# Graph convolution sums by ranked adding gathers in place of dense adjacency products

## The chip, the cores and the metric

The kernel runs on one core of a Trainium2 chip. TensorE (PE) multiplies matrices, VectorE (DVE) and ScalarE (ACT) do elementwise work, GpSimd (POOL) does elementwise work and issues indirect DMAs, SyncE (SP) issues most plain DMAs. The metric is the device time of one execution in microseconds (us). The kernel before takes 2163.23 us, the median of three runs (2161.73 to 2163.58).

## The reference

A small graph network over N = 2500 nodes with 256 features and E = 40000 directed edges, the edges sorted by their destination. Two blocks follow each other. The first adds a SAGE convolution (the mean over a node's incoming edges) and a linear attention to `x`, then a mixture of eight experts. The second is where the change lies: a two-layer GCN convolution and a stack of four linear-attention layers work on the same normalised rows, both are added to `x`, and a second mixture of experts closes the kernel.

```python
xn = _layernorm(x, axis=-1)
x = x + _L1_gnn_ref(xn, edge_index, ...) + _L1_mix_ref(xn[None], ...)[0]
x = x + _L1_ffn_ref(_layernorm(x, axis=-1)[None], ...)[0]
```

The GCN convolution, `_L1_gnn_ref`:

```python
def _gcn_aggregate(h, src, dst, norm, b, n):
    msg = h[src] * norm[:, None]
    agg = jax.ops.segment_sum(msg, dst, num_segments=n)
    return agg + b
n = x.shape[0]
loops = jnp.arange(n, dtype=edge_index.dtype)
src = jnp.concatenate([edge_index[0], loops])
dst = jnp.concatenate([edge_index[1], loops])
deg = jax.ops.segment_sum(jnp.ones_like(dst, dtype=x.dtype), dst, num_segments=n)
dis = jnp.where(deg > 0, jax.lax.rsqrt(jnp.maximum(deg, 1e-12)), 0.0)
norm = dis[src] * dis[dst]
h = _gcn_aggregate(x @ W1, src, dst, norm, b1, n)
h = jnp.where(h >= 0, h, alpha * h)
h = _gcn_aggregate(h @ W2, src, dst, norm, b2, n)
```

Each node sums the rows of its neighbours and its own row, scaled on both sides by `dis`, twice, with a product by a 256 x 256 matrix ahead of each sum.

## The kernel before

Nodes are cut into 20 tiles of 125 (`NT`, `P`), five groups of four tiles (`NG`, `GT`; a group has `GC` = 500 nodes). The work runs in stages, one after the other.

- **Loading and probing the edges**, to about 86 us of the span. `count_edges` gives each node its number of edges.
- **Build**, 86 to 305 us. For each group of destination nodes, one-hot products build the piece of the adjacency matrix (how often each of 2500 sources reaches each of the 500 nodes) in `edges`, in bf16. `neighbours` (line 292) multiplies it by the node table, which is held in three bf16 terms so that the sum is good to float32: 20 source tiles x 2 halves of 128 features x 3 terms = 120 matmuls of 374 ns for a group. A callback `between(k)` builds the next group's piece in between, and steps other generators (the routing's gates) along. The result is copied out by DVE and ACT (line 750, `aT`) and goes through the SAGE products. Here SP also writes each piece, with the identity added for the self loops (DVE, line 753), to `adj` in DRAM, 2500 x 2500 numbers in bf16.
- **Routing and the first mixture**, to 555 us: the tokens are scattered to their experts' rows of `sorted0` by POOL (line 407), and 47 tiles of 128 rows go through the experts from 356 us on (lines 813 to 850), 3.83 us each. SP loads each tile's expert weights (`wt`, four buffers) and rows (`xs`) ahead.
- **`first_norm`**, 555 to 628 us: layer-norm of all rows, and `conv_in`, the convolution's first 256 x 256 product scaled by `dis`. It writes the rows to `tab1` in DRAM and splits them in three bf16 terms (`split3`: ACT and POOL) to `table`.
- **Four attention layers**, `attention(l)`, 628 to 1678 us. Each computes keys, `context_out` (lines 982 to 1001), scores, and the feed-forward products `ffn(g)` for the five groups (lines 1148 to 1171). `conv_1(g)` (line 924) stands before `ffn` in these layers: groups 0 and 1 in layer 0, groups 2, 3 and 4 in layers 1, 2 and 3. It loads the pieces of `adj` on SP (four buffers, one DMA for two source tiles), does `neighbours`, scales by `dis` along the rows (`along_rows`, lines 273 to 282), applies the bias and the leaky unit, and does the second 256 x 256 product (`conv_in`, the products at line 914).
- **`conv_2`** (line 945), 1678 to 1813 us: the second sum, 600 matmuls with `adj` pieces again, transposed back and added to `X`.
- **Gates, sort and the second mixture**, to the end. The rows sorted for it lie in `sorted1`, which is an alias of `adj`'s memory; they are scattered by POOL (line 407) and gathered by POOL (line 1345).

Each engine runs its instructions in program order; the order across engines is set by semaphores that the tile framework places from the reads and writes of each buffer. If more edges fall on a place than a fixed window holds, `lost` is 1 and a loop of plain gathers computes the sums instead; the given edges don't need it.

Of the kernel before, what the change touches and what calls it, by code (L numbers as in the profile page):

```python
# [9 lines left out]
F32 = mybir.dt.float32  # L10
I32 = mybir.dt.int32
# [21 lines left out]
KC = 2  # L33
# [17 lines left out]
def gps_kernel(ctx: ExitStack, tc: tile.TileContext, a, out):  # L51
# [69 lines left out]
    ones = const.tile([P, 128], F32, name="ones")  # L121
    V.memset(ones, 1.0)
# [11 lines left out]
    adj = dram.tile([NG, P, NT, GC], BF16, name="adj")  # L134
    kth = scan.tile([128, 128], BF16, name="kth")
    G.iota(kth, pattern=[[1, 128]], base=0, channel_multiplier=0, allow_small_or_imprecise_dtypes=True)
    identb = scan.tile([P, P], BF16, name="identb")
    V.tensor_copy(identb, ident[:P, :P])
# [24 lines left out]
    begin = probe.tile([P, NQ], I32, name="begin")  # L163
# [47 lines left out]
    cnt = const.tile([P, NT], F32, name="cnt")  # L211

    def count_edges(pool):
# [15 lines left out]
        counts = dram.tile([N], F32, name="counts")  # L229
        nc.sync.dma_start(counts.rearrange("(q m n) -> m q n", q=NQ, n=BD), per)  # L230
        byrow = pool.tile([NT, P], F32, name="byrow")
        nc.sync.dma_start(byrow, counts.rearrange("(i p) -> i p", p=P))
        pc = psum2.tile([P, NT], F32, tag="cx", name="pc")
        T.transpose(pc, byrow, ident[:NT, :NT])
        V.tensor_copy(cnt, pc)
        return lost

    def gather_sums(pool, acc, table):
# [6 lines left out]
        gh = pool.tile([128, CH], F32, name="gh")  # L245
        V.tensor_scalar(gh, ge[:, :, 1], 1.0 / P, -0.496, ALU.mult, ALU.add)
        V.tensor_scalar(gh, gh, MAGIC, -MAGIC, ALU.add, ALU.add)
        gf = pool.tile([128, CH], F32, name="gf")
        V.tensor_copy(gf, ge[:, :, 1])
        V.scalar_tensor_tensor(gf, gh, -float(P), gf, ALU.mult, ALU.add)  # L250
        gs = pool.tile([128, CH], I32, name="gs")
        V.scalar_tensor_tensor(gs, gf, float(NT), gh, ALU.mult, ALU.add)
# [20 lines left out]
    def along_rows(pool, v, g):  # L273

        ps = psum2.tile([128, GC], F32, tag="ag", name="ps")
        for k in range(GT):
            dg = pool.tile([P, P], F32, tag="dg", name="dg")
            V.tensor_scalar(dg, ident[:P, :P], v[:, g * GT + k:g * GT + k + 1], None, ALU.mult)
            T.matmul(ps[:, k * P:(k + 1) * P], ones, dg, start=True, stop=True)
        row = pool.tile([128, GC], F32, tag="row", name="row")  # L280
        S.copy(row, ps)
        return row

    def neighbours(g, table, piece, between=None, banks=None):


        pa = banks or [psum2.tile([128, GC], F32, tag="ag", name=f"pa{c}") for c in range(2)]
        for k in range(NT):
            e = piece(k)
            for c in range(2):  # L290
                for n in range(3):
                    T.matmul(pa[c], table[:, k, n, c * 128:(c + 1) * 128], e,  # L292
                             start=(k == 0 and n == 0), stop=(k == NT - 1 and n == 2))
            if between is not None:
                between(k)
        return pa
# [238 lines left out]

    sorted1 = adj.rearrange("g p k d -> (g p k d)").bitcast(F32)[0:NE // 2 * N * RW].rearrange("(r c) -> r c", c=RW)
# [75 lines left out]
    with tc.tile_pool(name="lay0", bufs=1) as lay0:  # L612
# [91 lines left out]
        degrees(cnt)  # L704
# [5 lines left out]
        with tc.tile_pool(name="build", bufs=1) as build:  # L710
# [15 lines left out]

            ahead = new_edges()
            for k in range(GT):
                build_tile(ahead, 0, k)
            for g in range(NG):  # L730
                edges = ahead
                for lo, hi in ((0, g * GT), ((g + 1) * GT, NT)):
                    if hi > lo:
                        move(nc.sync, adj[g][:, lo:hi, :], edges[:, lo:hi, :])
# [5 lines left out]
                def between(k):  # L740
# [3 lines left out]
                    if gating is not None and k in (7, 15):  # L744
                        next(gating)

                pa = neighbours(g, xb, lambda k: edges[:, k, :], between)
# [3 lines left out]
                for k in range(GT):  # L751
                    o = edges[:, g * GT + k, k * P:(k + 1) * P]
                    V.tensor_tensor(o, o, identb, ALU.add)
                move(nc.sync, adj[g][:, g * GT:(g + 1) * GT, :], edges[:, g * GT:(g + 1) * GT, :])
# [22 lines left out]
    n_lost = nc.values_load(lost[0:1, 0:1], min_val=0, max_val=1)  # L777
    with tc.tile_pool(name="lost0", bufs=1) as pool, tc.For_i(0, n_lost, 1):
# [8 lines left out]
        nc.sync.dma_start(tab0.rearrange("(p k) d -> p k d", p=P), acc[:, :, :D])  # L787
# [78 lines left out]
    with tc.tile_pool(name="big", bufs=4) as big, tc.tile_pool(name="hid", bufs=8) as hid, \  # L866
# [30 lines left out]
        tab1 = dram.tile([N, D], F32, name="tab1")  # L897
        terms2 = dram.tile([NG, P, GT, 3, D], BF16, name="terms2")
        table = conv.tile([P, NT, 3, D], BF16, name="table")
        dval = const.tile([P, NT], F32, name="dval")  # L900
        V.tensor_scalar(dval, dis, valid, None, ALU.mult)

        def conv_in(g, src, w, keep):

            for b in range(0, GT, 2):
                i = g * GT + b
                if keep and b:
                    t = conv.tile([P, 3, D], F32, tag="t3", name="t3")[:, 0:2, :]
                else:
                    t = conv.tile([P, 2, D], F32, tag="t", name="t")  # L910
# [5 lines left out]
                if keep:  # L916
                    move(nc.sync, tab1.rearrange("(p k) d -> p k d", p=P)[:, i:i + 2, :], t)
                    split3(table[:, i:i + 2], t, G)
                else:
                    t3 = conv.tile([P, 2, 3, D], BF16, tag="t3", name="t3")  # L920
                    split3(t3, t, G)
                    move(nc.sync, terms2[g][:, b:b + 2], t3)

        def conv_1(g):
# [11 lines left out]
            for c in range(2):  # L936
                V.tensor_tensor(u[:, c, :], pa[c], row, ALU.mult)
# [551 lines left out]
```

## Time and profile before

| what | us |
|---|---|
| median of three runs | 2163.23 (2161.73 to 2163.58) |
| the profiled execution's own time | 2163.04 |
| its span | 2161.2 |
| mean granted clock of TensorE | 0.960 |
| layer 0 from `context_out` on, two groups of `conv_1` | 661.4 to 957.9 |
| layer 1 from `context_out` on, one group of `conv_1` | 957.9 to 1218.1 |
| layer 2 from `context_out` on, one group of `conv_1` | 1218.1 to 1478.3 |
| last group's `ffn` of layer 0, of layer 1, of layer 3 ends | 897.6, 1157.8, 1678.2 |
| `conv_2`'s matmuls | 1678.2 to 1807.2 |
| first product of the next stage (line 1254) | 1819.5 |

The profile counts from the first instruction. Its groups of instructions read: line, engine, operation, what it writes from what, and the count, then the busy time of all, the mean duration in ns, and the idle time of the engine just before them with what ended it. "issue" means that the profile shows nothing that the engine waited for. A clock of 1.00 is TensorE's full speed. A DMA that POOL issues shows as a POOL instruction of about 1 us; its data lands later.

### The profile page before, as it was taken

To read this page: it belongs to the slowest core of one execution; us is meant where nothing else is said; L and a number is where in the kernel's file an instruction comes from. 1 tells how busy PE (TensorE), PEld (TensorE's weight loads), DVE (VectorE), ACT (ScalarE), POOL (GpSimd) and SP (SyncE) were. 2 spreads that over 40 slices of the span, in tenths; PEclk is the share of its full clock that TensorE was granted. 3 is DMA by queue.
4 is the path that set the end of the run, shared out by engine and by line. 5 is a ranking of instruction groups with operands and counts; after the bars stand their busy time and mean duration, and the time that the engine had idled before them with its cause. 6 is when DMAs were issued, how large, how long until landed. Compare 5 with 4: busy or idle time off the path is not lost. (4 is left out here: it accounts for less than half of the span.)

```text
span 2161.2 us, 25307 instructions
## 1 busy us (share of the span) xinstructions
PE 1959.8 (91%) x9035; PEld 1309.3 (61%) x9035; DVE 896.2 (41%) x2822; ACT 580.8 (27%) x989; POOL 315.6 (15%) x288
## 2 busy tenths in 40 slices
PE   2699973999689999999999999999999998995996
PEld 2556643887466577676676767666676443334665
DVE  6866542333644346435463443635441023212333
ACT  1433201222361222223323133232322000331220
POOL 2302322222130201001010010000211000122222
PEclk9799986999799999999999999999999999997999
DMA  4022445665512200111001100022100435111100
GB/s 121 9 81 71 110 144 165 200 198 175 139 39 66 70 6 13 35 43 38 0 13 42 50 24 0 13 63 77 29 0 1 126 95 183 36 28 33 33 19 24
DMA packets 83119, 141.30 MB, mean 65 GB/s; under 512 B 18700, under 2 KB 64254, under 8 KB 82227
## 3 DMA queue, kind: packets, MB, share of 16 engines
q1 hardware_dynamic: 66193, 112.35, 17.7%
q0 software_dynamic: 13840, 20.89, 3.5%
q10 hardware_dynamic: 2949, 6.33, 1.1%
q8 instruction: 76, 1.25, 0.2%
q14 instruction: 61, 0.49, 0.1%
HBM read 103.85 MB, written 37.61 MB: 65 GB/s over the span
## 5 line engine op out<-in xcount | busy, mean ns | idle before, releaser
L1166 PE MATMUL mm<-w,h 128*125 128x256 f32 x1280 | 286.1, 379 | 0.0
L1156 PE MATMUL mm<-xT,w 128*128 128x500 f32 x640 | 282.9, 582 | 0.0
L1166 PEld LDWEIGHTS mm<-w,h 128*125 128x125 f32 x1280 | 239.2, 188 | 43.0 <-issue 9.2
L292 PEld LDWEIGHTS <-table 125*128 125x128 bf16 x1200 | 117.1, 98 | 126.7 <-issue 1.7
L1156 PEld LDWEIGHTS mm<-xT,w 128*128 128x128 f32 x640 | 119.0, 190 | 109.2 <-issue 100.8
L1159 ACT ACTIVATE h<-mm,bf 128x500 f32<-128x500 f32 x160 | 107.6, 677 | 216.6 <-PE mm L1156 216.5
L1151 POOL TENSOR_TENSOR tok<-tok,b 125x1024 f32<-125x1024 f32 x20 | 47.3, 2364 | 684.5 <-DVE tok L1143 632.4
L292 PE MATMUL pa<-piece,table 125*128 125x500 bf16 x600 | 138.1, 374 | 0.0
L292 PE MATMUL pa<-edges,xb 125*128 125x500 bf16 x600 | 134.4, 377 | 1.7 <-ACT edges L725 1.7
L292 PE MATMUL mm<-piece,table 125*128 125x500 bf16 x600 | 127.3, 374 | 0.0
L1167 DVE TENSOR_TENSOR tok<-tok,mm 125x256 f32<-125x256 f32 x80 | 33.5, 419 | 206.8 <-PE mm L1166 178.7
L1394 PE MATMUL py<-wd,taken 128*128 x432 | 96.9, 381 | 10.0 <-DVE taken L1384 10.0
L828 PE MATMUL mm<-xc,wt 128*128 128x128 f32 x752 | 97.1, 283 | 7.6 <-DVE idx L834 4.0
L828 PEld LDWEIGHTS mm<-xc,wt 128*128 128x128 f32 x752 | 89.6, 194 | 18.0 <-DVE xc L824 12.9
L292 PEld LDWEIGHTS <-xb 125*128 125x128 bf16 x600 | 58.2, 100 | 64.0 <-issue 4.1
L842 PE MATMUL py<-w,h 128*128 x376 | 96.1, 382 | 0.9 <-ACT h L832 0.9
L1394 PEld LDWEIGHTS py<-wd,taken 128*128 128x128 f32 x432 | 81.2, 190 | 25.3 <-DVE taken L1384 13.1
L832 ACT ACTIVATE h<-mm,wt 128x128 f32<-128x128 f32 x188 | 53.8, 369 | 137.6 <-issue 127.3
L357 ACT ACTIVATE xT<-mm,mixc 128x500 f32<-128x500 f32 x80 | 58.9, 768 | 116.1 <-PE mm L352 82.0
L725 ACT CAST edges<-mm 125x500 bf16<-125x500 f32 x100 | 64.7, 784 | 89.4 <-PE mm L722 80.3
L1254 PE MATMUL mm<-xTf,w 128*128 128x500 f32 x160 | 79.2, 618 | 6.0 <-DMA w<-in_L_ffn_W_dram 6.0
L1067 PE MATMUL mm<-xT,wa 128*128 128x500 f32 x160 | 76.4, 622 | 3.9 <-ACT xT L357 3.9
(363 smaller groups left out, 2833.6 us busy)
## 6 DMA issues: line engine op xcount, KB each, us to landing
wt<-in_expert_in_dram SPq DMA_DIRECT2D x47, 514.0 KB
piece<-adj SPq DMA_DIRECT2D x100, 218.8 KB
w<-in_L_mix_W_dram SPq DMA_DIRECT2D x8, 1024.0 KB
wd<-in_L_ffn_Wd_dram SPq DMA_DIRECT2D x8, 1024.0 KB
xs<-sorted SPq DMA_DIRECT2D x47, 130.0 KB
w<-in_L_ffn_W_dram SPq DMA_DIRECT2D x8, 512.0 KB
adj<-edges SPq DMA_DIRECT2D x2, 1750.0 KB
terms<-t SPq DMA_DIRECT2D x10, 336.0 KB
```

The source lines that it names most:

```text
L292: T.matmul(pa[c], table[:, k, n, c * 128:(c + 1) * 128], e, start=(k == 0 and n == 0), stop=(k == NT - 1 and n == 2))
L357: S.activation(o, ps, AF.Identity, bias=shift[:, c:c + 1], scale=gain[:, c:c + 1])
L725: S.copy(o.rearrange("p s (n d) -> p n s d", d=BD), ps[:P].rearrange("p (n s d) -> p n s d", n=BD, d=BD))
L828: T.matmul(ps[:, j * TS:(j + 1) * TS], wt[:, c * F0 + j * 128:c * F0 + (j + 1) * 128], xc[:, c * TS:(c + 1) * TS], start=(c == 0), stop=(c ...
L832: S.activation(h[:, j * TS:(j + 1) * TS], ps[:, j * TS:(j + 1) * TS], AF.Gelu, bias=wt[:, 2 * F0 + j:2 * F0 + j + 1])
L842: T.matmul(ps, h[:, j * TS:(j + 1) * TS], w2[:, ds(e, 1), j, :], start=(j == 0), stop=(j == NJ - 1))
L1067: T.matmul(ps, wk[:, kc, c * 128:(c + 1) * 128], hT[:, kc, g * GC:(g + 1) * GC], start=(kc == 0), stop=(kc == 1))
L1156: T.matmul(ps, w1[:, c, j * 128:(j + 1) * 128], fT[:, c, g * GC:(g + 1) * GC], start=(c == 0), stop=(c == 1))
L1159: S.activation(h, ps, AF.Gelu, bias=bf[:, l, j:j + 1])
L1166: T.matmul(ps, hh[j][:, k * P:(k + 1) * P], w2[:, j, :], start=(j == 0), stop=(j == nj - 1))
L1254: T.matmul(ps, w1[:, c, j * 128:(j + 1) * 128], xT[:, c, g * GC:(g + 1) * GC], start=(c == 0), stop=(c == 1))
L1394: T.matmul(ps, h[:, j * TS:(j + 1) * TS], wd[:, ds(e, 1), j, :], start=(j == 0), stop=(j == nj - 1))
```

## The change

The adjacency matrix is still built in `edges` for the first block, but no longer stored. The GCN sums are done by indirect DMAs that add in their destination.

`rank_nodes`, a generator stepped along in the build stage, ranks the nodes by their number of edges, the most first, by counts on DVE and two products for each group. Each node's number, its first edge and its `dis` are scattered to its rank's row of `byrank` (20 scatters on POOL), loaded back (`byr`), and 20 gathers bring the edges of each rank's node, as many as its tile's entry of `MOST`, to `wins`. `hit` tells which of them belong to the node; the others point to row N of the table, which is zero.

`gather` walks the 20 tiles of 128 ranked nodes, four at a time in turn. For each tile the first gather brings the nodes' own rows to `acc`, and each further one adds the row of one more neighbour: 20 plain and 349 adding gathers for one convolution by the sum of `MOST`. Each gather to a tile of `acc` waits for the tile's gather before it. `between(j)` then scales, adds the bias and applies the leaky unit; `to_nodes` scatters the tile's rows to the next table, `tabs[1]`, or to `sums2`. The second sum runs on rows before their product by `W2`, which `conv_out` does for all rows behind the layers. `conv_step(now)` places `between` in the programs of ACT and DVE: `LAYER` and `AHEAD` say how many gathers are reckoned to be done by a point of a layer, and every tile that is due by then is emitted there.

On DVE's program this puts three tiles' `between` after layer 0's third group, four at layer 0's end, four after the second and four after the fourth group of layer 1, four at its end, and the last after `context_out` of layer 2. On POOL it puts all 369 gathers of the first sum first, then the 20 scatters `to_nodes`, then the second sum's gathers.

Besides: `sorted1` has memory of its own, cleared by five SP DMAs from a tile of zeros (one stands ahead of the `lost` loop; four come in SP's order amid the first mixture's loads, two of them together after some 27 tiles, and one each four tiles later); the adds of `ffn` (lines 1151 and 1171) move from POOL to DVE; the loads of `b2` and `gm` move from POOL's queue to ACT's; the second fallback loop has its own flag `lost1`, one more value loaded to registers; the first fallback's table is laid out by node.

The core of the diff:

```diff
-KC = 2
+MOST = (42, 24, 22, 21, 20, 19, 18, 18, 17, 16, 16, 15, 15, 14, 14, 13, 13, 12, 11, 9)
+LAYER = 182
+AHEAD = 20
+NBIN = 64
...
-    adj = dram.tile([NG, P, NT, GC], BF16, name="adj")
...
+    def rank_nodes(pool):
+        bins = pool.tile([P, NBIN], F32, name="bins")
+        G.iota(bins, pattern=[[-1, NBIN]], base=NBIN - 1, channel_multiplier=0, allow_small_or_imprecise_dtypes=True)
+        upto = pool.tile([P, NT], F32, name="upto")
+        V.tensor_scalar(upto, cnt[:, 0:NT], float(NBIN - 1), None, ALU.min)
+        oh = pool.tile([P, NT, NBIN], F32, name="oh")
+        V.tensor_tensor(oh, bins[:, None, :].to_broadcast([P, NT, NBIN]), upto[:, :, None].to_broadcast([P, NT, NBIN]), ALU.is_equal)
+        full = pool.tile([128, NBIN], F32, name="full")
+        V.memset(full, 0.0)
+        rank = pool.tile([P, NT, NBIN], F32, name="rank")
...
+        at = pool.tile([P, NT], I32, name="at")
+        with nc.allow_low_precision("sums of one integer and zeros"):
+            V.tensor_reduce(at, rank, AX.X, ALU.add)
...
+        byrank = dram.tile([NT * 128, 4], F32, name="byrank")
...
+            made.append(G.indirect_dma_start(
+                out=byrank, out_offset=bass.IndirectOffsetOnAxis(ap=at[:, i:i + 1], axis=0), in_=rec[:, i, :], in_offset=None,
+            ))
...
+        byr = pool.tile([128, NT, 4], F32, name="byr")
+        nc.sync.dma_start(byr, byrank.rearrange("(j p) c -> p j c", p=128))
...
+        wins = pool.tile([128, heads_of[NT], 2], I32, name="wins")
+        hit = pool.tile([128, heads_of[NT]], F32, name="hit")
+        for j in range(NT):
+            part = slice(heads_of[j], heads_of[j + 1])
+            G.indirect_dma_start(
+                out=wins[:, part, :].rearrange("p e t -> p (e t)"), out_offset=None, in_=pairs,
+                in_offset=bass.IndirectOffsetOnAxis(ap=from_[:, j:j + 1], axis=0),
+            )
+            V.tensor_scalar(hit[:, part], wins[:, part, 0], byr[:, j, 0:1], None, ALU.is_equal)
...
-    sorted1 = adj.rearrange("g p k d -> (g p k d)").bitcast(F32)[0:NE // 2 * N * RW].rearrange("(r c) -> r c", c=RW)
+    sorted1 = dram.tile([NE // 2 * N, RW], F32, name="sorted1")
...
+            ranking = rank_nodes(build)
...
-                for lo, hi in ((0, g * GT), ((g + 1) * GT, NT)):
-                    if hi > lo:
-                        move(nc.sync, adj[g][:, lo:hi, :], edges[:, lo:hi, :])
...
+                    if g > 0 and k in (3, 11, 19):
+                        next(ranking, None)
...
-                    V.tensor_tensor(o, o, identb, ALU.add)
-                move(nc.sync, adj[g][:, g * GT:(g + 1) * GT, :], edges[:, g * GT:(g + 1) * GT, :])
...
-                if keep:
-                    move(nc.sync, tab1.rearrange("(p k) d -> p k d", p=P)[:, i:i + 2, :], t)
-                    split3(table[:, i:i + 2], t, G)
-                else:
-                    t3 = conv.tile([P, 2, 3, D], BF16, tag="t3", name="t3")
-                    split3(t3, t, G)
-                    move(nc.sync, terms2[g][:, b:b + 2], t3)
...
+                move(nc.sync, by_node(tabs[0])[:, i:i + 2, :], t)
...
-            row = along_rows(conv, dis, g)
-            pa = neighbours(g, table, piece)
-            u = conv.tile([128, 2, GC], F32, tag="u", name="u")
-            for c in range(2):
-                V.tensor_tensor(u[:, c, :], pa[c], row, ALU.mult)
-            for c in range(2):
-                neg = conv.tile([128, GC], F32, tag="row", name="neg")
-                V.tensor_scalar(neg, u[:, c, :], bcol[:, 0, c:c + 1], 0.0, ALU.add, ALU.min)
-                S.activation(u[:, c, :], u[:, c, :], AF.Relu, bias=bcol[:, 0, c:c + 1])
-                V.scalar_tensor_tensor(u[:, c, :], neg, alpha, u[:, c, :], ALU.mult, ALU.add)
-            conv_in(g, u, wc2, False)
...
+        def gather(tab, then, counted):
+            def one(j, k):
+                by = node[:, j:j + 1] if k == 0 else nbr[:, heads_of[j] + k - 1:heads_of[j] + k]
+                more = {} if k == 0 else {"compute_op": ALU.add}
+                counted()
+                return G.indirect_dma_start(out=acc[:, j, :], out_offset=None, in_=tab,
+                                            in_offset=bass.IndirectOffsetOnAxis(ap=by, axis=0), **more).ins
+            at = {j: 0 for j in range(4)}
+            coming = 4
+            wait = []
+            while at:
+                for j in list(at):
+                    ins = one(j, at[j])
+                    at[j] += 1
+                    wait = [(i, n - 1) for i, n in wait]
+                    while wait and wait[0][1] <= 0:
+                        then(wait.pop(0)[0])
+                    if at[j] > MOST[j]:
+                        del at[j]
+                        wait.append((j, 4))
+                        if coming < NT:
+                            at[coming] = 0
+                            coming += 1
+            for i, _ in wait:
+                then(i)
+            return ins
...
+        def to_nodes(tab, j):
+            G.indirect_dma_start(
+                out=tab, out_offset=bass.IndirectOffsetOnAxis(ap=node[:, j:j + 1], axis=0), in_=acc[:, j, :], in_offset=None,
+                bounds_check=N - 1, oob_is_err=False,
+            )
+        def between(j):
+            o = acc[:, j, :]
+            b = conv.tile([128, D], F32, tag="b", name="b", bufs=2)
+            S.activation(b, b1row, AF.Identity, scale=disr[:, 0, j:j + 1])
+            V.scalar_tensor_tensor(o, o, disr[:, 1, j:j + 1], b, ALU.mult, ALU.add)
+            neg = conv.tile([128, D], F32, tag="neg", name="neg", bufs=2)
+            V.tensor_scalar(neg, o, 0.0, alpha, ALU.min, ALU.mult)
+            V.scalar_tensor_tensor(o, o, 0.0, neg, ALU.max, ALU.add)
...
+            last["gather"] = gather(tabs[0], then, counted)
+        def conv_step(now):
+            while due and due[0][0] <= now:
+                j = due.pop(0)[1]
+                with tc.issue_after(last["add"]):
+                    between(j)
+                with tc.issue_after(last["gather"]):
+                    to_nodes(tabs[1], j)
+                if not due:
+                    gather(tabs[1], lambda j: to_nodes(sums2, j), lambda: None)
+        def conv_out(g):
+            s = conv.tile([P, GT, D], F32, tag="s", name="s", bufs=2)
+            move(nc.sync, s, by_node(sums2)[:, g * GT:(g + 1) * GT, :])
+            V.tensor_tensor(s, s, dval[:, g * GT:(g + 1) * GT, None].to_broadcast([P, GT, D]), ALU.mult)
+            sT = conv.tile([128, 2, GC], F32, tag="u", name="sT")
+            transpose_group(sT, 0, lambda k: s[:, k, :])
+            for b in range(0, GT, 2):
+                i = g * GT + b
+                ps = psum2.tile([P, 2, D], F32, tag="ag", name="ps")
+                for k in range(2):
+                    for c in range(2):
+                        T.matmul(ps[:, k, :], sT[:, c, (b + k) * P:(b + k + 1) * P], wc2[:, c, :], start=(c == 0), stop=(c == 1))
+                V.tensor_tensor(X[:, i:i + 2, :D], X[:, i:i + 2, :D], ps, ALU.add)
...
-                nc.gpsimd.dma_start(gm[:, h, :], row_bcast(a["L1_mix_bo"], l * D, D, 128))
+                nc.scalar.dma_start(gm[:, h, :], row_bcast(a["L1_mix_bo"], l * D, D, 128))
...
+                for n in range(0, 80, 16):
+                    nc.sync.dma_start(sorted1.rearrange("(p r) c -> p r c", p=P)[:, n:n + 16, :],
+                                      nothing[:, None, :].to_broadcast([P, 16, RW]))
...
+                first_sums()
...
+            conv_step(LAYER * l + AHEAD // 2)
...
-                G.tensor_tensor(o, o, b2[:P, None, :].to_broadcast([P, GT, D]), ALU.add)
+                V.tensor_tensor(o, o, b2[:P, None, :].to_broadcast([P, GT, D]), ALU.add)
...
-                    G.tensor_tensor(o, o, Y[:, g * GT:(g + 1) * GT, :D], ALU.add)
+                    V.tensor_tensor(o, o, Y[:, g * GT:(g + 1) * GT, :D], ALU.add)
...
-            for g in range(NG):
-                if max(g - 1, 0) == l:
-                    conv_1(g)
...
+                steps[nj + 3] = lambda g=g: conv_step(LAYER * l + AHEAD + (LAYER - AHEAD) * (g + 1) // NG)
...
-        conv_2()
+        with tc.issue_after(last["product"]), tc.issue_after(last["add"]):
+            for g in range(NG):
+                conv_out(g)
...
```

## The prediction

> **What bounds the kernel now.** I read the page's first two parts, its groups, the windows of single layers, and the timeline. PE is busy nearly throughout and POOL nearly idle; the 40 slices are 54 us each, and PE drops only at 324 to 378 us and in the last stages.
>
> ```profile
> span 2161.2 us, 25307 instructions
> PE 1959.8 (91%) x9035; PEld 1309.3 (61%) x9035; DVE 896.2 (41%) x2822; ACT 580.8 (27%) x989; POOL 315.6 (15%) x288
> ...
> PE   2699973999689999999999999999999998995996
> ...
> POOL 2302322222130201001010010000211000122222
> PEclk9799986999799999999999999999999999997999
> ```
>
> The convolutions are two groups of 600 matmuls: the first on `piece` (line 292, to `pa`) is the first convolution, to `mm` the second. The third group with 600 (`pa<-edges`) stays.
>
> ```profile
> L292 PE MATMUL pa<-piece,table 125*128 125x500 bf16 x600 | 138.1, 374 | 0.0
> ...
> L292 PE MATMUL mm<-piece,table 125*128 125x500 bf16 x600 | 127.3, 374 | 0.0
> ```
>
> The windows of the first two attention layers, with columns stretch, length, then busy time of PE, PEld, DVE, ACT, POOL, clock, show that PE alone sets a layer's length (259.32 of 260.20 us, clock 1.00):
>
> ```profile
> 661.40:957.90 296.50, 294.54 (x1257) 195.94 (x1255) 125.62 (x399) 82.83 (x122) 22.94 (x16) 1.00 0.13 37
> 957.90:1218.10 260.20, 259.32 (x1090) 178.29 (x1088) 117.86 (x387) 78.41 (x115) 18.18 (x12) 1.00 0.10 27
> ```
>
> So each removed PE microsecond in the layers shortens them, as long as no new wait appears. What replaces it runs on POOL. Its indirect DMAs, and back-to-back gathers of 128 rows in its timeline:
>
> ```profile
> L407 POOL DMA_INDIRECT sorted<-rows,to x40 | 48.0, 1200 | 159.9 <-issue 95.0 <-DVE to L402 45.7 <-DVE edges L753 19.2
> L848 POOL DMA_INDIRECT back<-yo,idx x47 | 45.9, 976 | 150.7 <-DVE yo L847 76.0 <-DVE idx L834 74.6
> ```
> ```profile
> 1967.06 0.96 POOL L1345 DMA_INDIRECT X<-adj,whence  x1 [0.31 <-issue]
> 1968.33 0.94 POOL L1345 DMA_INDIRECT X<-adj,whence  x1 [0.30 <-issue]
> 1969.58 0.95 POOL L1345 DMA_INDIRECT X<-adj,whence  x1 [0.30 <-issue]
> ```
>
> Each costs its 0.95 busy plus 0.30 of issue: starts are 1.254 us apart. A 125-row scatter (line 407, 1.20 busy) costs 1.50 the same way; a landing comes about 2.5 us after the start.
>
> **Step 1, what goes from the layers.** One group of the first convolution is 120 matmuls, 25.5 us, with 16 of line 914 and 8 of line 279: about 30.5 us. The windows agree: 296.5 has two groups, 260.2 one, 36.3 apart, of which some is the extra group's surroundings. Five groups: −152.5. The second convolution runs from 1678.2 to 1813; line 1254, the next stage's first matmul, starts at 1819.5. So bare layers end at 1678.2 − 152.5 = 1525.7. The 25 adds moved from POOL (lines 1151, 1171, 2.36 us) to DVE cost some 1.2 each there; DVE is 45% busy in a layer (117.86 of 260.20), so nothing.
>
> **Step 2, what POOL now needs.** Per convolution 20 plain gathers and 349 adding ones (the sum of `MOST`; the description says 367), and 20 scatters. No adding gather is in the trace. Nearest below: the plain gather, 1.254 of pitch. Nearest above: the 1.50 of line 407. Adding only changes what the DMA engines do (the destination is read as well), and rows are 128 of 1 KB as in line 1345, so I take 1.254. Four chains are interleaved, so an add waits for one issued 4 × 1.254 = 5.0 us earlier, twice the landing: no wait.
>
> The first gather can start when the last table write lands, T0 = 629.5 in the clock of before (the writes follow the layer-norm at 555 to 628). DVE and ACT must process each finished tile; these steps stand at fixed places of their programs. Layer 0's last place wants gather 177, done at T0 + 177 × 1.254 + 2.5 = T0 + 224.5; DVE is there at T0 + 207 (897.6 − 61 − 629.5): PE waits 17.5. Layer 1's last wants gather 363: T0 + 458, DVE 3.5 earlier. So PE's layers end at 1525.7 + 21 = 1546.7. The last tile's step stands behind `context_out` of layer 2, 60 us behind layer 1's end (1157.8 to 1218.1 before): T0 + 518. POOL has its 369 gathers and 19 scatters done at T0 + 487 and idles 31. Scatter and landing: the second convolution starts at T0 + 524. It needs 369 × 1.254 + 20 × 1.27 = 488, and 2.7 to land: T0 + 1015 = 1644.5. PE, out of layers at 1546.7, waits 98.
>
> Then `conv_out`: load and scale 6, five groups of PE work at 4.5 (16 matmuls of line 914's kind, 8 transposes), and about 4 of ramp at the lower clock after the wait: the next stage starts at 1677 instead of 1819.5: **−142**. A general pitch p gives T0 + 732 p + 97: each 0.01 us is 7.3 us.
>
> **Step 3, norm.** The three-way splits on POOL (40 at 1.16) and ACT leave the stage at 555 to 628, where DVE waits 13.9 us for POOL over five groups; the layer-norm stays. **−8**, between 0 and −14.
>
> **Step 4, ranking in the build stage.** It is new work in a chain: ranks on DVE, ready at about 237 us by its place among the groups (starts of the second to last group: 180, 221, 262); then 20 scatters of 125 rows at 1.50 = 30 and 2.5 to land; a load, 3; 20 gathers at 1.254 = 25 and 2.5; then `hit`, end 302.5. In DVE's order the 20 `hit`s stand ahead of the copy `aT` (old line 750) of the group that ends at 262.4, so it is 41 us late; PE needs its banks for the next group and waits. On POOL the routing scatters of line 407 queue behind the gathers too. Before, the barrier fell at 343.5, for a DMA that has gone, with the last scatters landed at about 339.6:
>
> ```profile
> 335.75 1.19 POOL L407 DMA_INDIRECT sorted<-rows,to  x1 [0.30 <-issue]
> 337.25 1.19 POOL L407 DMA_INDIRECT sorted<-rows,to  x1 [0.30 <-issue]
> ...
> 343.50 0.17 DVE L544 CAST ends<-fill 125x8 int32<-125x8 f32 x1 [17.50 <-DMA piece<-adj]
> ```
>
> 41 late minus that 4: **+37**. Bounds: −4 if the stalls are hidden; +42 if the 20 gathers cost 1.50 each as well.
>
> **Step 5, clearing `sorted1`.** Its rows get their own memory, cleared by five DMAs of 2000 packets of 1040 bytes, four of them on SP amid the first mixture's weight loads (`wt`, four buffers of 3.83 us a tile, so 11 to 15 us ahead). A 1040-byte packet takes 47 ns in the trace. On 16 engines a clear is 5.9 us: hidden, 0. The loads of 125 partitions at lines 617 and 618 show five late landings, as if on five engines: 18.8 us each, two back to back 37.6, so stalls of about 25 and twice 6 to 10: +37 to +49. I take **+30**, nearer to the landings. The Trainium skill ("DMA: Bandwidth & Descriptors", "Why a DMA increments its semaphore by 16 and not by 1") has it that the engines used are the largest number up to 16 that divides the outer sizes, five for 125, which speaks for the dear case: +43 there, 13 more in the sum.
>
> **Sum.** 2161.2 − 142 − 8 + 37 + 30 = 2078 of span; the profiled run, 2163.04, lies 1.84 above its span and 0.2 under the median. So 2080.
>
> **Rivals.**
> - *The adding gather is dearer (slower).* Place: POOL, pitch p of all but 40 of its gathers. Against it: all 20 plain gathers were busy 945 to 1131 ns. For: the operation isn't in the trace, line 407 has 1.50 with three rows less, and the 1131 fell in a stage with DVE's copies of 694 ns (line 1384). At 1.50, T0 + 1195: 2080 + 180 = 2260. It decides from p = 1.254 + 83/732 = 1.37; a 2% gain needs less than 1.31. PE then waits over 180 us. The skill's "SBUF — State Buffer" ("SBUF: two separate sides") warns of just this: some DVE copies lock GpSimd out of writing descriptors, and 620 ns become about 3100. If each of 732 gathers met one, that estimate adds 1800 us.
> - *Build and clears are hidden.* DVE's copy is not what PE waits for, and loads run ahead of the clears: steps 4 and 5 give −4 and 0, 2078 − 71 + 2 = 2009. For: PE is busy 9 tenths there and DVE not. Against: the fixed order.
> - *The chains wait for themselves.* An adding gather that lands after 6 us instead of 2.5 stretches four chains to 1.5 a gather: near 2260 again, with idle POOL and not busy POOL as the mark.
> - *Not what it says:* two passes of a fallback loop run if a tile's nodes have more edges than its entry of `MOST`. The given edges reach 32 at one node, under 42, and the other entries hold too. If it ran, 2 × 313 blocks of 128 edges with 20 products of some 0.374 us each would add over 4600.
>
> **How the numbers follow.** Forecast, pitch up to 1.37 and stalls taken: 0.45. Stalls hidden: 0.18. Pitch over 1.37: 0.25. Chains wait: 0.10. Fallback: 0.02. The likeliest's own range, 2040 to 2130 (step 5 from 0 to 49, p from 1.25 to 1.30). The range to hold 8 of 10: from 1995, under the hidden case, to 2245, two thirds into the dear one. Faster by over 0.2% (a measurement of this kernel can't tell less from no change): 0.62; within: 0.03, the border of the first and third case; slower: 0.35, these two, the chains and the fallback.
>
> **What would show it.** Right: POOL busy over 70% of the layers; adding gathers near 0.95 us and 1.25 apart; layers of about 230 us; a PE wait of 98 us before the last convolution's products, at half clock behind it; a hole of 30 to 40 us in PE at 262; five clears at 19 us each. Wrong: a pitch over 1.37, idle of POOL on its own landings, or PE not waiting at all.

## The result, and the profile after

The changed kernel takes 2713.8 us, the median of four runs (2711.37 to 2716.89), against 2162.61 before in the same comparison: a ratio of 1.2549, 95% interval 1.2528 to 1.2571. 2080 was forecast, with 2245 as the upper end. The first two parts of its page:

```profile
span 2710.6 us, 23424 instructions
...
PE 1751.2 (65%) x7817; PEld 1218.0 (45%) x7817; DVE 926.9 (34%) x2922; ACT 556.7 (21%) x954; POOL 1413.5 (52%) x1030
...
PE   3799429656989380389967998810000069998797
...
POOL 1215422111288888888874888888888800002221
PEclk8799769878999695689988999865555579999899
```

A slice is now 68 us. PE has 209 us less work and the span is 549 longer: POOL is busy through the middle, and for five slices, from about 1830 to 2170 us, PE does nothing, at half clock. Two of its groups (busy us and mean ns, then idle time and what ended it):

```profile
L1009 POOL DMA_INDIRECT acc<-tab,nbr x698 | 1087.1, 1558 | 214.8 <-issue 211.2
L1284 PE MATMUL mm<-w,h 128*125 128x256 f32 x1280 | 287.8, 381 | 421.2 <-DMA w<-in_L_mix_W_dram 421.2
```

The first is the 698 adding gathers: 1558 ns each, not the 950 of a plain one, and 0.30 of issue (211.2 over 698), so 1.86 from start to start. The second is one wait of 421 us, in the feed-forward products of layer 3, for weights. The forecast's sum, term by term, from the landmarks of both traces:

| stretch | before | after | difference | forecast |
|---|---|---|---|---|
| start to first expert product (lines 828, 905) | 358.0 | 406.9 | +49 | +37 |
| expert products, first to last start | 188.7 | 244.3 | +56 | +30 |
| from there to the first gather (before: T0) | 82.8 | 76.9 | −6 | −8 |
| first gather to the load of the second sums | | 1455 | | 1015 |
| that load to the next stage's first product (lines 1254, 1372) | | 191 | | 32 |
| from there to the end | 341.7 | 336.7 | −5 | 0 |

Against the forecast the rows are +40 (the first three), +440, +159 and −5, together 634: 2080 + 634 = 2714.

### The profile page after: what moved, and what is told of

Its sections match the earlier page's. It is cut to its first block, busy times and chain, and to the rows that moved or that the text cites. A ratio compares the mean times of both kernels' runs of the same rounds, so it can differ in the third digit from the quotient of the medians.

```text
span 2710.6 us, 23424 instructions
## 1 busy us (share of the span) xinstructions
PE 1751.2 (65%) x7817; PEld 1218.0 (45%) x7817; DVE 926.9 (34%) x2922; ACT 556.7 (21%) x954; POOL 1413.5 (52%) x1030
## 5 line engine op out<-in xcount | busy, mean ns | idle before, releaser
L1009 POOL DMA_INDIRECT acc<-tab,nbr x698 | 1087.1, 1558 | 214.8 <-issue 211.2
L1274 PE MATMUL mm<-xT,w 128*128 128x500 f32 x640 | 290.6, 597 | 0.9 <-ACT xT L439 0.9
L925 POOL DMA_INDIRECT back<-yo,idx x47 | 45.9, 976 | 228.3 <-DVE idx L911 126.8
L1277 ACT ACTIVATE h<-mm,bf 128x500 f32<-128x500 f32 x160 | 106.8, 677 | 225.1 <-PE mm L1274 224.0
L489 POOL DMA_INDIRECT sorted<-rows,to x40 | 49.1, 1228 | 147.6 <-issue 97.0
L1247 PE MATMUL po<-gm,qt 128*125 128x256 f32 x320 | 81.5, 400 | 54.5 <-ACT qt L96 46.0
L1183 PEld LDWEIGHTS mm<-xT,wa 128*128 128x128 f32 x160 | 30.4, 202 | 168.9 <-ACT xT L439 144.1
L1247 PEld LDWEIGHTS po<-gm,qt 128*125 128x125 f32 x320 | 62.8, 199 | 79.6 <-ACT qt L96 50.2
L1520 POOL DMA_INDIRECT out_dram<-yo,idx x27 | 27.0, 1001 | 135.4 <-DVE yo L1519 117.1
L489 POOL DMA_INDIRECT sorted<-X,to x20 | 23.8, 1192 | 136.8 <-DVE to L484 132.2
```

The costliest lines, as they stand in the source:

```text
L489: moved.append(G.indirect_dma_start(out=table, out_offset=bass.IndirectOffsetOnAxis(ap=to[:, k:k + 1], axis=0), in_=rows[:, k, :], in_offs ...
L1009: return G.indirect_dma_start(out=acc[:, j, :], out_offset=None, in_=tab, in_offset=bass.IndirectOffsetOnAxis(ap=by, axis=0), **more).ins
L1183: T.matmul(ps, wk[:, kc, c * 128:(c + 1) * 128], hT[:, kc, g * GC:(g + 1) * GC], start=(kc == 0), stop=(kc == 1))
L1247: T.matmul(po[:, b * D:(b + 1) * D], qt[:, 2 * b + c, :], gm[:, c, :], start=(c == 0), stop=(c == 1))
L1274: T.matmul(ps, w1[:, c, j * 128:(j + 1) * 128], fT[:, c, g * GC:(g + 1) * GC], start=(c == 0), stop=(c == 1))
L1277: S.activation(h, ps, AF.Gelu, bias=bf[:, l, j:j + 1])
```

## The experiments

**e1_plain: the price of adding.**

```diff
-                more = {} if k == 0 else {"compute_op": ALU.add}
+                more = {}
```

> Every gather of a neighbour is plain and overwrites its tile instead of adding to it, so the sums are left out; count, indices, rows and chains stay. Theory (the adding form itself costs POOL 0.59 us more, 1.54 busy against 0.95): the 698 gathers fall to about 0.95 busy, 1.25 apart, and the time by 732 x 0.61 = 444 us to about 2270; SP's block of layer 3's weights stays. Rival (the index tile of the neighbours, or waits in the chains, make them slow): 1.5 busy stays and so does 2714. Rival (DVE holds POOL up): 1.5 stays in the layers and falls only where DVE rests.

Measured 2362.68. The group of the same 698 gathers:

```profile
L1009 POOL DMA_INDIRECT acc<-tab,nbr x698 | 674.9, 967 | 215.7 <-issue 210.3 <-DMA acc<-tab,nbr 5.0 <-DMA sums<-acc,node 0.3
```

967 instead of 1558 ns, with the same indices, rows and chains: the price is that of adding. That is 698 x 0.591 = 412 us of POOL's time (the 444 expected charged the plain gathers as well), and the kernel is 351 us faster. Most of the other 61 is POOL waiting: for DVE, at the scatters between the two sums, 65.1 us in e1 and 7.5 in the changed kernel. e12 below shows where that comes from. The rival on DVE's copies falls in the changed kernel's own trace: in the 250 us in which PE, DVE and ACT do nothing at all, POOL starts an indirect DMA every 1.77 us (141 of them, scatters among them) as in the stretch before (1.83), where all are busy. The adding gathers among them take 1.542 us on average in the idle stretch and 1.565 in the busy one:

```profile
1800.00:2050.00 250.00, 0.00 (x0) 0.00 (x0) 0.00 (x0) 0.00 (x0) 207.35 (x141) 0.50 0.50 73
1500.00:1800.00 300.00, 250.82 (x983) 175.19 (x981) 126.43 (x408) 78.14 (x114) 250.31 (x164) 0.92 0.53 80
```

(Columns: stretch, length, busy us of PE, PEld, DVE, ACT and POOL with counts, clock, DMA share, GB/s.)

**e7_half: what the price goes by.** The first sum's gathers bring 64 rows, the second's bring rows of 512 bytes; W2's load stands ahead as in e2.

```diff
-                return G.indirect_dma_start(out=acc[:, j, :], out_offset=None, in_=tab,
+                if tab is tabs[0]:
+                    return G.indirect_dma_start(out=acc[:64, j, :], out_offset=None, in_=tab,
+                                                in_offset=bass.IndirectOffsetOnAxis(ap=by[:64], axis=0), **more).ins
+                return G.indirect_dma_start(out=acc[:, j, :128], out_offset=None, in_=tab.rearrange("n (h d) -> (n h) d", h=2),
```

> Changed kernel with layer 3's W2 load ahead of the second sums' loads; gathers of the first sum bring 64 rows instead of 128, those of the second bring rows of 512 bytes instead of 1024 (so both sums are left incomplete). It measures what the 0.59 us of an adding gather go by. Theory (POOL's work per row, whatever its length): 64 rows fall to 0.75 to 0.95 busy, 512-byte rows stay at 1.54. Rival (bytes, the destination read as well): 512-byte rows fall to about 1.25 and 64 rows likewise. Rival (a fixed price per instruction): both stay near 1.54. The plain gathers of the same sizes show the same for 0.95.

Measured 2523.68, with e2's edit in it; what counts here is the price of one gather. The groups of adding gathers (`nbr`; line 1013 has the 512-byte rows, line 1011 the 64 rows), the group of plain gathers of 64 rows (`node`), and one plain and one adding gather of 64 rows from the timeline (start, duration):

```profile
L1013 POOL DMA_INDIRECT acc<-tab,nbr x349 | 544.3, 1560 | 108.0 <-issue 104.8 <-DMA acc<-tab,nbr 3.2
L1011 POOL DMA_INDIRECT acc<-tab,nbr x349 | 500.9, 1435 | 106.3 <-issue 99.0 <-DMA acc<-tab,nbr 7.3
...
L1011 POOL DMA_INDIRECT acc<-tab,node x20 | 18.7, 934 | 77.3 <-DMA tab<-t 71.5 <-DMA acc<-tab,nbr 3.4 <-issue 2.4
```
```profile
742.83 0.91 POOL L1011 DMA_INDIRECT acc<-tab,node  x1 [0.30 <-issue]
...
751.71 1.42 POOL L1011 DMA_INDIRECT acc<-tab,nbr  x1 [0.31 <-issue]
```

Half the bytes change nothing, half the rows 0.12 us. On average a plain gather of 64 rows takes 0.93 (0.97 with 128, e1) and an adding one 1.43 (1.56): most of it is a price of the instruction, and adding raises it by 0.50 with 64 rows and 0.59 with 128. Both the theory of a price per row and that of bytes fell; fewer rows than 64 were not tried.

**e2_sp_order: the wait for weights.** In the changed kernel's SP queue (start, duration, what is issued):

```profile
1661.52 0.37 SPq L593 DMA_DIRECT2D w<-in_L_mix_W_dram  x1
2183.02 1.74 SPq L88 DMA_DIRECT2D s<-sums  x4
2184.92 0.39 SPq L593 DMA_DIRECT2D w<-in_L_mix_W_dram  x1
```

The last line is layer 3's W2. Four loads of `conv_out` stand ahead of it and wait for the last scatter of the second sum; `tc.issue_after(last["product"])` and `tc.issue_after(last["add"])` hold back what follows on PE and on DVE, nothing on SP. PE, on its timeline, stops at layer 3's first W2 product:

```profile
1766.02 5.19 PE L1274 MATMUL mm<-xT,w 128*128 128x500 f32 x12
2192.41 5.34 PE L1284 MATMUL mm<-w,h 128*125 128x256 f32 x16 [421.20 <-DMA w<-in_L_mix_W_dram]
```

The edit:

```diff
-            w2 = load_w(weights("w2"), a["L1_mix_W2"][l], D)
+            w2 = weights("w2").rearrange("p (c n) -> p c n", n=D)
+            last["w2"] = nc.sync.dma_start(w2, a["L1_mix_W2"][l].rearrange("(c p) n -> p c n", p=128)).ins
...
-        with tc.issue_after(last["product"]), tc.issue_after(last["add"]):
+        with tc.issue_after(last["product"]), tc.issue_after(last["add"]), tc.issue_after(last["w2"]):
```

> The loads of the second sums are queued on SP behind layer 3's W2 load instead of ahead of it; nothing else changes. Theory (the block on SP, not POOL alone, sets layer 3's end): PE's wait of 421 us at line 1284 goes, layer 3 runs beside the gathers, line 1372 starts some 32 us behind the last landing at 2183 instead of 191, so 158 less: about 2556. Rival (POOL's gathers alone set the end and PE would have waited anyway): the same 2714.

Measured 2559.07, 155 less. W2 is now loaded at 1727.59, and PE waits 274 us at the end of the layers, for the sums: POOL's own time, which was forecast as 98.

**e3_clear16: the clears.** PE in the changed kernel's first mixture waits three times behind them:

```profile
549.33 0.82 PE L899 MATMUL px<-ident,xs 128*128 128x128 f32 x2 [32.64 <-DMA xs<-sorted]
577.01 0.66 PE L899 MATMUL px<-ident,xs 128*128 128x128 f32 x2 [11.11 <-DMA xs<-sorted]
605.37 0.66 PE L899 MATMUL px<-ident,xs 128*128 128x128 f32 x2 [10.92 <-DMA xs<-sorted]
```

```diff
-                for n in range(0, 80, 16):
-                    nc.sync.dma_start(sorted1.rearrange("(p r) c -> p r c", p=P)[:, n:n + 16, :],
-                                      nothing[:, None, :].to_broadcast([P, 16, RW]))
+                for n in range(0, 125, 25):
+                    nc.sync.dma_start(sorted1.rearrange("(p r) c -> p r c", p=80)[:, n:n + 25, :],
+                                      nothing[:80, None, :].to_broadcast([80, 25, RW]))
```

> The five clears of sorted1 are laid out as 80 outer rows instead of 125, the same bytes and packets. Theory (125 outer rows keep a clear to 5 of 16 engines, 18.8 us each, and the loads of the first mixture queue behind them): a clear spreads over 16 engines, 5.9 us, the first mixture falls from 246 us to about 200 of 196 before, the time by 40 to 50 us to about 2668. Rival (the bytes of the clears as such, or the gathers' tables, hold the loads up): under 15 us.

Measured 2655.23, 59 less. The expert products take 192.2 us from the first to the last start (244.3 with 125 outer rows, 188.7 before the change), and the first of them starts 7 us earlier (400.0, 406.9 in the changed kernel). In a window of 170 us PE works 161 at clock 0.99, where the changed kernel had 130 in 180 at 0.87:

```profile
420.00:590.00 170.00, 161.03 (x1067) 141.34 (x1066) 55.03 (x165) 46.57 (x164) 39.95 (x41) 0.99 0.76 231
```

As many packets and bytes, and the wait is gone: the layout did it. The rule of the Trainium skill for the count of engines ("DMA: Bandwidth & Descriptors", "Why a DMA increments its semaphore by 16 and not by 1"), the largest number up to 16 that divides the outer sizes, gives five for 125 and sixteen for 80, which agrees with this. The 43 that the prediction worked out for five engines is nearer to the 52 that went (244.3 to 192.2) than the 30 that was taken.

**e4_rank_late and e8_rank_early: the ranking.** e4 puts only the 20 `hit`s behind the copy `aT` of group 3.

> The 20 compares hit stand behind group 3's copy aT on DVE instead of ahead of it. Theory (DVE's order makes PE wait 37 us in the build stage): PE's hole before line 838 goes, the last scatter to sorted0 starts 25 to 40 us earlier than 381, and the time falls by as much, to about 2680. Rival (POOL's queue, where the routing scatters stand behind 20 scatters and 20 gathers of the ranking, sets the barrier): the last scatter moves by less than 12 us.

Measured 2713.92: nothing; the last routing scatter starts at 378.5 instead of 381.0. DVE's timeline of e4 tells why:

```profile
275.08 0.18 DVE L309 TENSOR_SCALAR from__2382<-byr 128x20 int32<-128x20 f32 x1 [23.06 <-DMA byr<-byrank]
...
302.12 0.34 DVE L330 CAST whose<-wins 128x349 f32<-128x349 int32 x1 [24.48 <-DMA wins<-in_edges_dram,from__2382]
302.38 0.67 DVE L834 COPY aT<-pa 128x500 f32<-128x500 f32 x1
```

Two other instructions of the ranking wait there for DMAs, `from_` for 23 us and `whose` for 24.5, and `aT` is still behind both. e8 starts the ranking one group earlier and puts all three behind an `aT`:

```diff
-                    if g > 0 and k in (3, 11, 19):
+                    if k in (3, 11, 19):
...
+        yield
+        yield
+        with tc.issue_after(rank_nodes.copied):
             V.tensor_scalar(from_, byr[:, :, 1], float(E), None, ALU.min)
```

> Of the changed kernel only the ranking is moved: it begins one group earlier, and its steps on DVE that wait for DMAs (the use of byr, the compares, the copy of wins) stand behind the copy aT of the group. Theory (DVE's waits for the ranking's DMAs, 23 and 24 us, hold up aT and with it PE): PE's hole of 37 us goes, the first tile of the mixture starts 30 to 45 us earlier than 405.7, the time is about 2675. Rival (POOL's queue: 40 DMAs ahead of the routing scatters): less than 12 us.

Measured 2693.91, 20 less, between the two. PE's hole is gone (its longest wait between 200 and 330 us is 4.2), the last routing scatter starts at 359.9 instead of 381.0, against 337.2 before the change, and the first expert product at 386.6 instead of 406.9. The other half of the delay stays. POOL's 40 DMAs ahead of the routing scatters and DVE's ranking may both have part in it; that was not tried.

**e5_plain_sp and e12_plain_again: the forecast's own pitch.** Edits of e1 and e2 together.

> Both edits together: plain gathers that overwrite (the sums are left out) and the second sums' loads behind layer 3's W2 load. This is the pitch that was forecast, without the block that was not. By the forecast's sum with the 40 us that its steps 3 to 5 came out dearer: 2120. By the run with plain gathers alone, whose last sums landed at about 1830: 1830 + 32 + 337, so 2200; the difference of 80 is then a wait of POOL between the two sums that step 2 mis-sized (scatters that wait for each other, the last tile's step later than T0 + 518). Rival (one of the two edits makes the other useless): 2363 or more.

This kernel took 3011.58, with all engines but POOL waiting in steps of 5.6 us for nothing that the profile names. The same kernel was run again.

> The very kernel with plain gathers and the loads behind W2's once more, since 3011 came out where 2200 was expected. Theory (that execution was a slow one, its engines waited in steps of 5.6 us for nothing that the profile names): 2190 to 2210. Rival (it belongs to the program): 3011 again.

2216.64, the median of 2215.17 and 2218.1, with a ratio of 1.0252 (1.0231 to 1.0273). What held up the one execution of 3011 is not known, and nothing is read from it. So with the pitch that was forecast and no block the change would still be slower. The first sum's gathers take 471 us from T0, the first gather's start (463 forecast). Then POOL's timeline:

```profile
1268.32 0.97 POOL L1033 DMA_INDIRECT tab<-acc,node  x1 [2.18 <-DVE y L388]
1271.50 0.97 POOL L1033 DMA_INDIRECT tab<-acc,node  x1 [2.21 <-DVE kmax L1185]
1327.02 0.97 POOL L1033 DMA_INDIRECT tab<-acc,node  x1 [54.54 <-DVE acc L1046]
1330.03 0.98 POOL L1009 DMA_INDIRECT acc<-tab,node  x1 [2.04 <-DMA tab<-acc,node]
```

The scatters stand 3.2 us apart, each after the landing of the one ahead (1.3 in e6 below, where they are declared independent), and the last waits 54.5 us for a DVE step behind `context_out` of layer 2: it starts at T0 + 597, where 520 was forecast. Of these 77 us, 47 are lost by the end of layer 0, where DVE waits for a gather and PE behind it:

```profile
1001.04 0.88 DVE L1043 SCALAR_TENSOR_TENSOR acc<-acc,disr,b 128x256 f32<-128x256 f32 x2 [49.51 <-DMA acc<-tab,nbr]
1003.18 4.43 PE L1183 MATMUL mm<-xT,wa 128*128 128x500 f32 x6 [48.87 <-ACT xT L439]
```

DVE is there at T0 + 222 and goes on at T0 + 271; the forecast was T0 + 224.5, as gather 177 lands. It counted the gathers in the order of the source, and POOL's queue has another: in the traces of e12 and of the changed kernel the plain gathers, each of which begins a tile, stand at places 1 to 5, 15, 40 and 127, where the source's walk has 1 to 4, 92, 96, 104 and 174. The wait ends as about the 211th gather lands, here, in e1 and in the changed kernel (there after 106.8 us). The other 30 us are lost behind it, most of them in layer 1: it takes 257 us from `context_out` to `context_out`, where 233 was forecast, and no step in it waits for a gather. Why it is no shorter is the next run.

**e10_cut: what the first convolution's products were worth.** The kernel before, with one source tile of 20 in `conv_1`.

```diff
-            pa = neighbours(g, table, piece)
...
+            e = piece(0)
+            for c in range(2):
+                for n in range(3):
+                    T.matmul(pa[c], table[:, 0, n, c * 128:(c + 1) * 128], e, start=(n == 0), stop=(n == 2))
```

> The kernel before, with the first convolution's sums cut to one of 20 source tiles (114 of 120 products of each of five groups left out, and 9 of 10 loads of adjacency pieces); all else stays. It measures step 1 by itself. Forecast's step 1 (each removed microsecond of PE shortens its layer): 5 x 114 x 0.212 = 121 less, 2041. Rival (those products filled PE's waits at the seams of a layer, where DVE normalises rows; without them some 17 us of waits and a lower clock show in each layer): 30 to 60 less, 2100 to 2130.

Measured 2124.01: 38 less for 121 us of products left out. In the kernel before, PE's timeline at a seam of two layers has those products between all the others:

```profile
924.71 3.33 PE L292 MATMUL pa<-piece,table 125*128 125x500 bf16 x15
928.13 0.70 PE L1089 MATMUL mm<-ident,xT 128*125 128x128 f32 x4
928.67 2.06 PE L292 MATMUL pa<-piece,table 125*128 125x500 bf16 x9
...
952.86 0.80 PE L292 MATMUL pa<-piece,table 125*128 125x500 bf16 x3
```

Without them the waits show, here at the start of layer 3 in e10, and its window of one layer:

```profile
1415.39 1.22 PE L1093 MATMUL mm<-ident,xT 128*125 128x128 f32 x4 [5.16 <-ACT xT L1084]
...
1454.95 0.65 PE L1124 MATMUL mm<-ident,q 125*128 125x125 f32 x4 [2.86 <-DVE q L1118]
1470.32 1.97 PE L352 MATMUL mm<-ident,tok 125*128 125x125 f32 x8 [7.28 <-DVE tok L1147]
```
```profile
891.20:1156.20 265.00, 250.03 (x1001) 177.42 (x1001) 120.69 (x393) 82.03 (x122) 23.26 (x16) 0.96 0.09 26
```

15 us of waits, and 1001 products that take 250 us at a mean clock of 0.96, where 1090 took 259 at 1.00: this stretch, from the first such product of layer 1 to that of layer 2, has 89 products fewer than the layer of 260.2 us shown before, and is no shorter. From `context_out` to `context_out`, as in the table of the kernel before, layers 0, 1 and 2 take 262, 267 and 258 us (296, 260 and 260 before), and the rest to the last feed-forward product 193 (200). So only layer 0, which had two groups, got much shorter. PE at 99% was a PE with filler.

**e6_fixes: all mended, still adding.** e2, e3 and e8, scatters of `to_nodes` declared independent, `LAYER` 122 and `AHEAD` 16.

> Adding gathers as in the changed kernel, with all that was found mended: the loads behind W2's, clears over 80 outer rows, the ranking a group earlier with its steps behind the copies aT on DVE, scatters of to_nodes that don't wait for each other, and places for 122 gathers a layer instead of 182. Theory (POOL's 698 adding gathers at 1.86 alone now set the end): start at about 632, 698 x 1.86 + 80 x 1.26 = 1400, then 32 and 337: about 2403, still slower than before. Rival (the stalls, not the gathers, made the loss): under 2200.

Measured 2546.07, 143 over the expectation. The first sum's gathers end at 1323, but the last scatters wait for DVE steps that the new constants put too late:

```profile
1401.99 0.97 POOL L1043 DMA_INDIRECT tab<-acc,node  x1 [55.55 <-DVE acc L1060]
...
1467.43 0.97 POOL L1043 DMA_INDIRECT tab<-acc,node  x1 [60.46 <-DVE acc L1060]
```

These two account for 116 of the 143. Neither number was met; that POOL sets the end holds (PE waits 521 us for the sums).

**e9_hybrid and e11_hybrid2: only the first sum by gathers.** The second stays dense, the adjacency is stored again, `sorted1` is its alias again. The core:

```diff
+        def conv_mid(g):
+            s = conv.tile([P, GT, D], F32, tag="s", name="s")
+            move(nc.sync, s, by_node(tabs[1])[:, g * GT:(g + 1) * GT, :])
...
+                V.tensor_copy(t, ps)
+                split3(table[:, i:i + 2], t, V)
```

> A new kernel: the first convolution by ranked adding gathers, the second by dense products as before (the adjacency stored again, sorted1 in its memory again, so no clears); the rows come back from DRAM in layer 3, go through W2 and the three-way split while the last groups of layer 3 run. Theory (349 adding gathers, 20 plain and 20 scatters, 700 us of POOL, hide under the 917 us of the layers without the first convolution's 152 us of PE): 2162 - 152 + 22 of PE for the products + 10 to 30 for the ranking: about 2050, faster than before. Rival (the gathers slow the layers, by DVE's steps or by their DMAs, or the ranking costs as much as it saves): 2100 to 2170.

2168.73, in the rival's range, with a ratio of 1.0036 (1.0021 to 1.0051). The 369 gathers do hide: they end at 1327, and the layers at about 1679. But a layer is as long as ever:

```profile
911.70:1169.20 257.50, 236.88 (x944) 166.61 (x944) 124.29 (x393) 76.44 (x114) 214.54 (x142) 0.96 0.54 86
```

944 products instead of 1090, and 257.5 us instead of 260.2. e11 moves the ranking beside the first mixture and the steps between the sums to other places.

> The kernel with the first sum by gathers and the second dense, mended where its first version lost time: the whole ranking runs beside the first mixture, two of its POOL DMAs for each tile, its flag is read at the end; places of the steps between the sums by the times of the run before; the rows' way through W2 stands where layer 3 waits for DVE. Theory (17 us of the first version went to the ranking in the build stage and 20 to the products of W2 in a busy place): 2169 - 37 = 2130, faster than before. Rival (the ranking costs the mixture as much, and PE's waits at the seams stay): 2160 to 2170.

2193.31, ratio 1.0142 (1.0118 to 1.0166): worse than e9, and outside both expectations. The first expert product starts 27 us earlier (354.0, 381.4 in e9), but the expert products take 212.8 us from first to last start (188.3 in e9), so the ranking costs 24 there. And PE waits 12.7 and 15.2 us in the first two layers for ACT, which waits 72 us in all for DVE, at steps that now seem to stand ahead of their gathers. No version here beats the kernel before. e10 gives the likely reason, by which none of this kind would by much: with 114 of 120 products of each group left out, 38 us are to be had (the smaller products and steps of the first sums stay in e10 and are not in this number), and the ranking took 23 of them in e9 (its first expert product starts at 381.4, before at 358.0).

## Why the prediction was wrong

- **Step 2, the pitch of an adding gather, failed.** "Adding only changes what the DMA engines do", so 1.254 was taken, and 1.50 was held for the upper bound. It is 1.86 (1.558 busy and 0.30): adding costs POOL itself 0.59 us an instruction (e1), whatever the rows' length (e7). A row of another operation was no bound from above, so neither was 2260. By the prediction's own 732 p + 97 the sums end at T0 + 1459 with 1.86; measured 1455. That this is so close is in part luck: with the pitch that was forecast the formula gives T0 + 1015, and e12 has T0 + 1111.
- **Step 2 also took POOL's order from the source.** The wait at layer 0's end, priced at 17.5 us for gather 177, is 49.5 in e12 and 106.8 in the changed kernel, for about the 211th. In the changed kernel it costs little, since POOL waits only 7.5 us for DVE at the scatters there; with the forecast's own pitch it is 47 of the 77 us by which the second sum starts late.
- **The queue on SP was not priced.** `conv_out`'s loads were costed as 6 us of latency, and what stands behind them on SP was never named. It was layer 3's W2, 155 us (e2).
- **Step 1 failed as well, hidden by the others.** That "each removed PE microsecond in the layers shortens them" gave −152; for 121 us of it e10 gives 38. The condition "as long as no new wait appears" was written beside it and then not examined. In e12 it makes up most of the other 30 us of lateness at `context_out` of layer 2, for which POOL waits between the sums.
- **Step 5** had the mechanism right (five engines) and the size low: 56 (52 by e3) against 30, above even the upper bound of 49.
- **Step 4** had the place right: `aT` at 304.1 against 303.4. The total was 49 for 37; the last scatter began 44 us later than before. The 4 taken off for the old barrier should have been 2: the last routing scatter of before lands at about 341, not 339.6 (337.25, and about 4 to land, as this group's landings in e10's trace).
- **Step 3** was right: −6 for −8.
- **The rivals.** The one on the slower side was right in kind, POOL's pitch with the point at 1.37, and far too mild; neither of its hints, line 407's price and DVE's copies, was the cause. Chains that wait for themselves: 3.7 us in all. DVE locking POOL out: not seen (1.565 us a gather with DVE busy, 1.542 with it idle). Stalls in build and clears hidden: not so.

## What to carry to other kernels

Before an instruction is issued 700 times in place of something else, run it twenty times: no row of another form bounds its price. An engine that is busy all the time in a long stage may be kept so by the very work that is to go; leave that work out and measure before counting on its time. And name for each DMA that waits what stands behind it in its queue, for every queue: ordering that holds on two engines holds nothing on the third. A place counted in the order of the source is a guess until a trace shows the queue's own order.

## What was not expected of the hardware

An indirect gather costs POOL nearly the same whether it brings 64 or 128 rows (0.93 and 0.97 us plain, 1.43 and 1.56 adding), and the same with 512 or 1024 bytes a row (1.56 both, adding): for the most part the instruction is paid for, not the data. And clears of 2000 packets of zeros each hold up the loads beside them with 125 outer rows (the expert products take 55.6 us longer than before) and hardly with 80 (3.5).
